# The MLP's first weights above the projection's buffers and ahead of its tables; three engines in program order to the MLP's end

## The chip, the cores and the metric

The kernel runs on one core of a Trainium2 chip. The metric is device time in microseconds (us), the median of a few runs. Beside it stands one profiled execution, whose trace lists every instruction on every engine with its start and its length.

The engines are named as the profile names them: PE is TensorE (matrix products, and transposes by a product with an identity), DVE is VectorE, ACT is ScalarE, POOL is GpSimd, SP is SyncE, which here does nothing but ask for DMA transfers. Each engine runs its own instruction list in order and waits at semaphores for the others. A "q" after an engine's name (DVEq, SPq) is its sequencer: branches, waits and requests for transfers. PSUM is the memory that PE writes its results into; a bank holds the result of one product.

## The reference

Two layers on an image of 48 x 48 tokens (2304) with 768 channels, all in float32. Layer 0 is a transformer block; layer 1 is a spectral mixing layer:

```python
# layer 0
xn = layernorm(x, ln1_g, ln1_b)
q, k, v = split(xn @ qkv_w + qkv_b)              # 12 heads of 64
attn = softmax(q*scale @ k^T + rel_h + rel_w)    # relative position along rows and columns
x = x + (attn @ v) @ proj_w + proj_b
h = gelu(layernorm(x, ln2_g, ln2_b) @ mlp_w1 + mlp_b1)      # 768 -> 3072
x = x + h @ mlp_w2 + mlp_b2                                 # 3072 -> 768
# layer 1
xf = rfft2(x, norm="ortho")                      # over the 48 x 48 tokens
o1 = relu(xf * w1 + b1); o2 = softshrink(o1 * w2 + b2, 0.01)  # complex, 8 blocks of 96 channels
y = irfft2(o2, norm="ortho") + x
```

The change touches the second half of layer 0: the projection `@ proj_w` with its residual, the second layer norm, and the MLP.

## The kernel before, in words

**Stages.** The program goes through layer norm with q, k and v, then attention, the projection, the MLP, and the spectral layer. The result of the first half, x1, stays on the chip as 18 tiles of 128 tokens. A program of this kind is written in Python as a list of operations with tiles from pools. A pool with `bufs=2` gives the same tile name two buffers in turn, and a third request waits for the last reader of the first. Pools opened inside a `with` give their memory back when it ends; a later pool that is laid in that memory waits for the readers of what was there. By default a scheduler decides the order of the instructions of each engine; inside `tc.manual_schedule(engines=...)` the engines named keep the order in which the program is written.

**Products by sevens.** Large products are done on 2 x 2 blocks with seven block products where eight are usual, at the price of sums of the operands. The helpers `left` (L158 to L168 with `right`) make the four sums of a left or right operand: `t1 = b12 - b11`, `t2 = b22 - t1` and so on. They run on GpSimd for the MLP's weights, on VectorE for its activations (`hs`), and on VectorE for the projection's activations (`sums_of_outputs`) and for the tokens that go into the MLP (`sums_of_tokens`, L170 to L177).

**The projection** (`projected`, L794 to L836). It goes over nine pairs u of token tiles. The attention's result `og` for a pair comes by DMA (`outputs`, L755). PE makes seven products of three matmuls each (L810) into four PSUM banks. ScalarE copies the first (pm1), VectorE adds it to the second (pu, L828) and the third (pu7, L832), GpSimd adds pu and pu7 into x1 (`first`, L820), and VectorE adds the other four products into x1 (`into`, L823). Pairs 0 to 3 run while a flag is tested that says whether the attention's short form of the softmax was safe. The branch on it is at L898. Pairs 4 to 8, the late projection, come after it. There the second layer norm of the first six token tiles is done too (`normalise`, L121 to L129: statistics on VectorE, a square root on ScalarE, then VectorE), their transposes (`transposed`: PE at L139, three transposes to a PSUM buffer, two buffers, read by ScalarE at L141 and VectorE at L145 in turn), and the addition of the MLP's second bias by GpSimd. The scheduler is free in all of this.

**The MLP.** Three passes p over 768 tokens each, and in a pass 12 blocks n of 256 hidden features. `hidden(p, n)` loads the block's w1 (L1147) and w2 (L1154, 768 KB each) by requests on SP, has GpSimd make the sums of both (eight operations), and makes seven products into four PSUM banks `h0` to `h3` (L1170). ScalarE copies the first (m1, L1189), VectorE adds (u, u7 and three c, L1182), ScalarE applies GELU (L1176), and VectorE makes the four sums `hs` of the result. `added(p, n, i)`, for three token groups i, makes seven single products with w2 (L1230, L1234) into banks `o0` to `o3`, which VectorE adds into x1 and into an accumulator (L1232 to L1238). The weights come from a pool with two buffers. The second half of block n-1, `added(p, n-1, i)`, is written between the parts of `hidden(p, n)`. The layer norm of the next pass's six tiles (`normalised`) is written at blocks 4 to 9; at the end of a pass come its transposes (`turned`), `sums_of_tokens` and the first step of the Fourier transform (`rows_forward`, L1262 to L1275). All of the MLP holds PE to program order; the other engines are free. Ahead of the first weights SP asks for two tables, b2 (L1133) and rows_dft (L1135).

Of the kernel before, what the change touches and what calls it, by code (L numbers as in the profile page):

```python
# [10 lines left out]
F32 = mybir.dt.float32  # L11
# [8 lines left out]
P = 128  # L20
HW = 48
T = HW * HW
# [7 lines left out]
TB = 768  # L30
G = 384
# [15 lines left out]
def block_then_afno(  # L47
# [26 lines left out]
    nc = tc.nc  # L74
# [39 lines left out]
    xt = shared[:, : NC * TB].rearrange("p (c t) -> p c t", c=NC)  # L114
# [78 lines left out]
    with ExitStack() as flag_scope:  # L193
# [557 lines left out]
        def outputs(u, pool, og=None):  # L751

            if og is None:
                og = pool.tile([P, NC, 2, P], F32, name="og", bufs=2)
            nc.sync.dma_start(  # L755
                out=og.rearrange("p c j t -> p c (j t)"),
                in_=oT[:, ts(u, 2 * P)].rearrange("(c p) t -> p c t", p=P),
            )
            return og
# [35 lines left out]
        def projected(psum, pool, u, og, sums):  # L795

            b11, b21, t3, b22 = (og[:, ds(3 * i, 3), j] for j in range(2) for i in range(2))
            t1, t2, t4 = (sums[:, i] for i in range(3))
            a11, a12, s3, a22 = weight_parts()
            s1, s2, s4 = (pws[:, i] for i in range(3))  # L800
            pairs_of = {
                1: (b11, a11), 2: (b21, a12), 3: (b22, s4), 4: (t4, a22),
                5: (t1, s1), 6: (t2, s2), 7: (t3, s3),
            }
            bank = [psum.tile([P, G], F32, name=f"m{i}") for i in range(4)]

            def product(i, k, first):
                a, b = pairs_of[k]
                for c in range(3):
                    nc.tensor.matmul(  # L810
                        bank[i], a[:, c, :], b[:, c, :], start=(first and c == 0),
                        stop=(c == 2), skip_group_check=not first,
                    )
                return bank[i]

            def half(j, k):
                return x1[:, 2 * u + j, ts(k, CH)]

            def first(j, k, src):
                nc.gpsimd.tensor_tensor(half(j, k), half(j, k), src, ALU.add)  # L820

            def into(j, k, src):
                nc.vector.tensor_tensor(half(j, k), src, half(j, k), ALU.add)  # L823

            m1 = pool.tile([P, G], F32, name="pm1")
            nc.scalar.copy(m1, product(0, 1, True))
            v = pool.tile([P, G], F32, name="pu")
            nc.vector.tensor_tensor(v, product(1, 6, True), m1, ALU.add)  # L828
            first(0, 1, v)
            first(1, 0, v)  # L830
            v7 = pool.tile([P, G], F32, name="pu7")
            nc.vector.tensor_tensor(v7, product(2, 7, True), v, ALU.add)  # L832
            first(1, 1, v7)
            into(1, 1, product(3, 5, True))
            into(0, 0, product(0, 2, False))
            into(0, 1, product(2, 4, False))  # L836
            into(1, 0, product(3, 3, False))
# [60 lines left out]
        with tc.If(safe < 1):  # L898
# [178 lines left out]
            with tc.tile_pool(name="g_ps_proj", bufs=2, space=PSUM) as psum, tc.tile_pool(  # L1077
# [9 lines left out]
                for i in range(4):  # L1087
                    sum_of_weights(i)

        with tc.tile_pool(name="ps_proj", bufs=1, space=PSUM) as psum, tc.tile_pool(  # L1090
            name="ps_turn", bufs=2, space=PSUM
        ) as psum_turn, tc.tile_pool(name="proj_late", bufs=2) as pl:
            hats, ogs = [], {EARLY: sums_of_outputs(pl, kept[EARLY])}
            for u in range(EARLY, PAIRS):
                if u + 1 < PAIRS:
                    if u + 1 not in kept:
                        kept[u + 1] = outputs(u + 1, pl)
                    ogs[u + 1] = sums_of_outputs(pl, kept[u + 1])
                projected(psum, pl, u, kept[u], ogs.pop(u))
                n = u - EARLY  # L1100
                if n in (2, 3):
                    transposed(
                        psum_turn, hats[3 * (n - 2) :][:3], xt, n - 2, V_LN2G, V_LN2B, tag="t"
                    )
                if n == 3:
                    sums_of_tokens(xt, xs)
                if n < 3:
                    for t in (2 * n, 2 * n + 1):
                        hats.append(normalise(ln2, x1[:, t, :]))
                        nc.gpsimd.tensor_tensor(x1[:, t, :], x1[:, t, :], b2, ALU.add)  # L1110
# [19 lines left out]
    with ExitStack() as mlp:  # L1130
        bias = mlp.enter_context(tc.tile_pool(name="mlp_const", bufs=1))
        b2 = bias.tile([P, C], F32, name="b2")
        nc.sync.dma_start(out=b2, in_=mlp_b2[0, :].partition_broadcast(P))  # L1133
        rows_dft = bias.tile([P, 3, 8, 64], F32, name="rows_dft")
        nc.sync.dma_start(out=rows_dft, in_=c_rows)  # L1135

        psum = mlp.enter_context(tc.tile_pool(name="ps_mlp", bufs=1, space=PSUM))
        hpool = mlp.enter_context(tc.tile_pool(name="mlp_h", bufs=2))
        upool = mlp.enter_context(tc.tile_pool(name="mlp_u", bufs=2))
        wpool = mlp.enter_context(tc.tile_pool(name="mlp_w", bufs=2))  # L1140
        n_f = FF // FCH
        kept = {}

        def hidden(p, n):

            w = wpool.tile([P, NC, FCH], F32, name="w1")
            nc.sync.dma_start(  # L1147
# [11 lines left out]
                nc.gpsimd, v[:, 0, :CH], v[:, 0, CH:], v[:, 1, :CH], v[:, 1, CH:],  # L1159
                [vs[:, i] for i in range(3)],  # L1160
            )
            h = hpool.tile([P, 2, TB], F32, name="hT")
            hs = hpool.tile([P, 3, G], F32, name="hs", bufs=1)
            kept[p, n] = h, hs, v, vs
# [116 lines left out]
        def normalised(p, i):  # L1281

            t = 6 * p + i
            hats[i] = turn.tile([P, C], F32, name="hat2", tag="turn")
            normalise(upool, x1[:, t, :], hats[i])
            nc.gpsimd.tensor_tensor(x1[:, t, :], x1[:, t, :], b2, ALU.add)  # L1286

        def turned(piece):

            for i in range(4 * piece, 4 * piece + 4):  # L1290
                j, c = divmod(i, NC)
                tp = psum.tile([P, G], F32, name="tp2", tag=f"h{i % 4}")
                for k in range(3):
                    nc.tensor.transpose(tp[:, ts(k, P)], hats[3 * j + k][:, ts(c, P)], ident)
                nc.scalar.activation(
                    xt[:, c, ts(j, G)], tp, AF.Identity, bias=col(V_LN2B + c), scale=col(V_LN2G + c)
                )

        with tc.manual_schedule(engines={mybir.EngineType.PE}):
            for p in range(T // TB):  # L1300
                for n in range(n_f):
                    work = hidden(p, n)
                    for i in range(3):
                        next(work)
                        if n:
                            added(p, n - 1, i)
                    if p < 2 and 4 <= n < 10:
                        normalised(p + 1, n - 4)
                for i in range(3):
                    if p < 2:  # L1310
                        turned(i)
                    added(p, n_f - 1, i)
                if p < 2:
                    sums_of_tokens(xt, xs)
                rows_forward(p)

    with ExitStack() as sp:
        psum = sp.enter_context(tc.tile_pool(name="ps_spec", bufs=2, space=PSUM))
# [380 lines left out]
```

## Time and profile before

| | us |
|---|---|
| median of three runs (2856.51 to 2860.92) | 2859.09 |
| profiled execution | 2857.95 |
| its span, first instruction to last | 2856.1 |
| PE busy | 2797.9 |
| DVE busy | 1734.3 |
| ACT busy | 915.6 |
| POOL busy | 651.7 |

PE's mean granted clock is 0.996 of full speed. By stage, from the windows view of the trace:

| stretch of the span, us | stage | PE busy |
|---|---|---|
| 0 to 480 | layer norm, q, k, v | 460.5 |
| 480 to 1430 | attention | 950 |
| 1430 to 1492.3 | projection of pairs 0 to 3, flag | 57.8 |
| 1492.3 to 1566.5 | late projection, pairs 4 to 8 | 73.9 |
| 1566.5 to 1576.3 | border to the MLP | 0.06 |
| 1576.3 to 1601.3 | first blocks of the MLP | 24.1 |
| 1601.3 to 2570 | the rest of the MLP | 963.0 |
| 2570 to 2856.1 | spectral layer | 268.5 |

How to read the profile: a row of instructions has the source line, the engine and operation, and the tiles it writes and reads as `out<-in` with their sizes. A row in brackets, `[9.74 <-DMA w]`, gives the idle time ahead of the instruction on its engine and what ended it. The list of waits gives, for each kind of waiting instruction and its releaser, the total, the number of times and the longest. Matmuls overlap, so three matmuls that make one product are best counted from the start of one product to the start of the next. The records' names of PE's matmuls into `h`, `o` and `m` are the PSUM banks of the MLP's first half, its second half, and the projection.

### The profile page before, as it was taken

What the parts mean: (1) busy time and instruction counts of PE and PEld (TensorE: products, weight loads), DVE (VectorE), ACT (ScalarE), POOL (GpSimd) and SP (SyncE); (2) the same over time, 40 slices, a digit from 0 to 9 for tenths busy, and PEclk for the clock granted to TensorE, in tenths of its full rate; (3) what the DMA queues carried; (4) which work ended last, traced back from release to release, by engine and by line L of the source; (5) the groups of instructions that cost most, each with busy time, mean ns of one, the idle gap of its engine ahead of it and who ended that gap; (6) DMA issues with size and microseconds to landing.
All of it is one profiled execution on the core that took longest, in us unless ns stands there. A gap on an engine that the chain in (4) does not pass through costs nothing. (4 is left out here: it accounts for less than half of the span.)

```text
span 2856.1 us, 41310 instructions
## 1 busy us (share of the span) xinstructions
PE 2797.9 (98%) x15829; PEld 1724.1 (60%) x15829; DVE 1734.3 (61%) x2540; ACT 915.6 (32%) x1470; POOL 651.7 (23%) x650
## 2 busy tenths in 40 slices
PE   8999999999999999999999999999999999999998
PEld 5555655656566656565555555555555555556887
DVE  5343226666666666676756666675666566666665
ACT  1011125657566666565501101121011211102332
POOL 2303010000000000000063532242232323222433
PEclk9999999999999999999999999999999999999999
DMA  4423275374573736546240221121121212113254
GB/s 150 132 99 111 93 164 108 62 134 79 88 141 52 135 60 113 115 73 100 94 175 21 85 66 59 52 91 62 46 67 56 89 56 66 49 61 112 61 161 141
DMA packets 216494, 262.79 MB, mean 92 GB/s; under 512 B 24524, under 2 KB 196908, under 8 KB 214752
## 3 DMA queue, kind: packets, MB, share of 16 engines
q1 hardware_dynamic: 213784, 258.03, 36.4%
q8 instruction: 127, 2.08, 0.3%
q10 hardware_dynamic: 2440, 1.84, 0.2%
q14 instruction: 79, 0.65, 0.1%
q0 software_dynamic: 64, 0.20, 0.0%
HBM read 143.96 MB, written 52.31 MB: 69 GB/s over the span
## 5 line engine op out<-in xcount | busy, mean ns | idle before, releaser
L581 ACT ACTIVATE main<-sp 128x768 f32<-128x768 f32 x648 | 516.5, 812 | 34.0 <-PE sp L571 19.3
L725 DVE TENSOR_TENSOR pairs<-pairs,main 128x1536 f32<-128x1536 f32 x252 | 443.1, 1758 | 27.2 <-DVE pairs L725 0.9
L571 PE MATMUL sp<-terms,select 64*128 64x384 f32 x1296 | 413.5, 630 | 0.0
L1232 DVE TENSOR_TENSOR main<-o,main 128x384 f32<-128x384 f32 x540 | 298.5, 556 | 39.5 <-PE o L1230 1.7
L1170 PE MATMUL h<-shared,w 128*128 128x384 f32 x864 | 298.0, 488 | 9.7 <-DMA w<-in_mlp_w_dram 9.7
L562 PE MATMUL sp<-shared 64*128 64x384 f32 x1296 | 266.9, 487 | 2.2 <-DVE o L462 2.2
L562 PE MATMUL sp<-qT,kT 64*128 64x384 f32 x1296 | 264.1, 484 | 0.0
L451 PE MATMUL m<-main 128*128 128x384 f32 x756 | 246.8, 488 | 2.7 <-DVE main L177 2.1
L1170 PEld LDWEIGHTS h<-shared,w 128*128 128x128 f32 x864 | 164.6, 191 | 125.9 <-POOL main L1286 10.3
L1170 PE MATMUL h<-shared,w1s 128*128 128x384 f32 x648 | 226.8, 486 | 0.4 <-POOL w1s L160 0.4
L627 POOL TENSOR_TENSOR inverse<-inverse,rden 24x32 f32<-24x32 f32 x36 | 15.2, 422 | 929.1 <-DVE sums L626 887.5
L1176 ACT ACTIVATE hT<-c,vec 128x384 f32<-128x384 f32 x108 | 66.4, 615 | 477.1 <-DVE c L1182 477.1
L594 PE MATMUL op<-main,shared 128*64 128x384 f32 x1296 | 217.4, 488 | 0.0
L594 PE MATMUL op<-main,v 128*64 128x384 f32 x1296 | 216.4, 488 | 0.0
L725 DVE TENSOR_TENSOR pairs<-main 128x1536 f32<-128x1536 f32 x36 | 63.3, 1758 | 247.3 <-ACT main L581 247.3
L451 PEld LDWEIGHTS m<-main 128*128 128x128 f32 x756 | 143.4, 191 | 103.7 <-issue 4.8
L1182 DVE TENSOR_TENSOR c<-h,u 128x384 f32<-128x384 f32 x108 | 60.2, 558 | 218.4 <-PE h L1170 218.4
L1230 PE MATMUL o<-w2s,hs 128*128 128x384 f32 x432 | 174.9, 487 | 2.3 <-DVE hs L160 2.3
L571 PEld LDWEIGHTS sp<-terms,select 64*128 64x128 f32 x1296 | 126.1, 187 | 83.7 <-issue 0.5
L1230 PE MATMUL o<-w,hT 128*128 128x384 f32 x432 | 175.1, 487 | 1.4 <-DVE acc L1238 0.7
L1170 PEld LDWEIGHTS h<-shared,w1s 128*128 128x128 f32 x648 | 123.0, 190 | 86.7 <-POOL w1s L160 1.2
L159 POOL TENSOR_TENSOR w1s<-w 128x384 f32<-128x384 f32 x36 | 36.9, 1024 | 547.0 <-DMA w<-in_mlp_w_dram 416.4
(187 smaller groups left out, 4033.8 us busy)
## 6 DMA issues: line engine op xcount, KB each, us to landing
w<-in_mlp_w_dram SPq DMA_DIRECT2D x72, 768.0 KB
terms<-col_parts SPq DMA_DIRECT2D x432, 72.0 KB
terms<-row_hi SPq DMA_DIRECT2D x216, 72.0 KB
terms<-row_lo SPq DMA_DIRECT2D x216, 72.0 KB
main<-in_qkv_w_dram SPq DMA_DIRECT2D x36, 384.0 KB
z<-zt SPq DMA_DIRECT2D x48, 192.0 KB
x<-in_x_blocks_dram SPq DMA_DIRECT2D x18, 384.0 KB
k_d<-o SPq DMA_DIRECT2D x36, 192.0 KB
```

The lines of the kernel that those rows point to most:

```text
L159: eng.tensor_tensor(s[0], a21, a22, ALU.add)
L451: nc.tensor.matmul(bank, a[:, c, :], b[:, c, :], start=(first and c == 0), stop=(c == 2), skip_group_check=not first,)
L562: nc.tensor.matmul(sp[:, j, :G], kT[at, ts(kt, P)], qT[at, ts(c, G)], start=first, stop=not first,)
L571: nc.tensor.matmul(sp[:, j, :G], select[at, a % 2], ready[pr, c][at, a // 2, b], start=first, stop=not first,)
L581: nc.scalar.activation(p, sp[:, :, :G], AF.Exp, scale=HD**-0.5)
L594: nc.tensor.matmul(op[ts(j, 64)], v[:, kt, ts(j, 64)], exps[:, kt, j, :], start=(kt == 0), stop=(kt == NT - 1),)
L725: nc.vector.tensor_tensor(pairs, so_far, exps[:, ds(kt - 1, 2)], ALU.add)
L1170: nc.tensor.matmul(bank[i], a[:, c, :], b[:, c, :], start=(start and c == 0), stop=(c == 2), skip_group_check=not start,)
L1176: nc.scalar.activation(h[:, i, ts(k, G)], src, AF.Gelu, bias=col(V_B1 + 2 * n + i))
L1182: nc.vector.tensor_tensor(t, src, other, ALU.add)
L1230: nc.tensor.matmul(bank[k], a, b, start=start, stop=True, skip_group_check=not start)
L1232: nc.vector.tensor_tensor(dst, bank[k], dst, ALU.add)
```

## The change

Five edits. In the late projection pm1, pu and pu7 get one buffer each in place of two, and `og` of u = 6 to 8 comes from the pool `pj` (which also holds u = 4 and 5, two buffers) and no longer from `proj_late`. A manual schedule of PE, POOL and SP opens ahead of the late projection and closes behind the MLP, in place of the one of PE alone around the MLP. A pool `apart` with one tile that nobody uses is put below the weights' pool, so that this pool lies above the projection's buffers. The loads and sums of a block's weights leave `hidden` for a function `weights(p, n)`; it is called for (0, 0) ahead of the loop, for the next block behind the products of a block, and for the first two blocks of the next pass behind `sums_of_tokens`. The requests for b2 and rows_dft move from ahead of the MLP to block (0, 2).

```diff
--- before.py
+++ after.py
@@ -822,13 +822,13 @@
             def into(j, k, src):
                 nc.vector.tensor_tensor(half(j, k), src, half(j, k), ALU.add)
 
-            m1 = pool.tile([P, G], F32, name="pm1")
+            m1 = pool.tile([P, G], F32, name="pm1", bufs=1)
             nc.scalar.copy(m1, product(0, 1, True))
-            v = pool.tile([P, G], F32, name="pu")
+            v = pool.tile([P, G], F32, name="pu", bufs=1)
             nc.vector.tensor_tensor(v, product(1, 6, True), m1, ALU.add)
             first(0, 1, v)
             first(1, 0, v)
-            v7 = pool.tile([P, G], F32, name="pu7")
+            v7 = pool.tile([P, G], F32, name="pu7", bufs=1)
             nc.vector.tensor_tensor(v7, product(2, 7, True), v, ALU.add)
             first(1, 1, v7)
             into(1, 1, product(3, 5, True))
@@ -1087,6 +1087,12 @@
                 for i in range(4):
                     sum_of_weights(i)
 
+        in_order = ExitStack()
+        in_order.enter_context(
+            tc.manual_schedule(
+                engines={mybir.EngineType.PE, mybir.EngineType.Pool, mybir.EngineType.SP}
+            )
+        )
         with tc.tile_pool(name="ps_proj", bufs=1, space=PSUM) as psum, tc.tile_pool(
             name="ps_turn", bufs=2, space=PSUM
         ) as psum_turn, tc.tile_pool(name="proj_late", bufs=2) as pl:
@@ -1094,7 +1100,7 @@
             for u in range(EARLY, PAIRS):
                 if u + 1 < PAIRS:
                     if u + 1 not in kept:
-                        kept[u + 1] = outputs(u + 1, pl)
+                        kept[u + 1] = outputs(u + 1, pj)
                     ogs[u + 1] = sums_of_outputs(pl, kept[u + 1])
                 projected(psum, pl, u, kept[u], ogs.pop(u))
                 n = u - EARLY
@@ -1130,18 +1136,20 @@
     with ExitStack() as mlp:
         bias = mlp.enter_context(tc.tile_pool(name="mlp_const", bufs=1))
         b2 = bias.tile([P, C], F32, name="b2")
-        nc.sync.dma_start(out=b2, in_=mlp_b2[0, :].partition_broadcast(P))
         rows_dft = bias.tile([P, 3, 8, 64], F32, name="rows_dft")
-        nc.sync.dma_start(out=rows_dft, in_=c_rows)
 
         psum = mlp.enter_context(tc.tile_pool(name="ps_mlp", bufs=1, space=PSUM))
         hpool = mlp.enter_context(tc.tile_pool(name="mlp_h", bufs=2))
         upool = mlp.enter_context(tc.tile_pool(name="mlp_u", bufs=2))
+        apart = mlp.enter_context(tc.tile_pool(name="apart", bufs=1))
+        apart.tile([P, 560], F32, name="apart")
         wpool = mlp.enter_context(tc.tile_pool(name="mlp_w", bufs=2))
         n_f = FF // FCH
         kept = {}
 
-        def hidden(p, n):
+        ready_w = {}
+
+        def weights(p, n):
 
             w = wpool.tile([P, NC, FCH], F32, name="w1")
             nc.sync.dma_start(
@@ -1159,6 +1167,11 @@
                 nc.gpsimd, v[:, 0, :CH], v[:, 0, CH:], v[:, 1, :CH], v[:, 1, CH:],
                 [vs[:, i] for i in range(3)],
             )
+            ready_w[p, n] = a11, a12, a21, a22, ws, v, vs
+
+        def hidden(p, n):
+
+            a11, a12, a21, a22, ws, v, vs = ready_w.pop((p, n))
             h = hpool.tile([P, 2, TB], F32, name="hT")
             hs = hpool.tile([P, 3, G], F32, name="hs", bufs=1)
             kept[p, n] = h, hs, v, vs
@@ -1296,23 +1309,31 @@
                     xt[:, c, ts(j, G)], tp, AF.Identity, bias=col(V_LN2B + c), scale=col(V_LN2G + c)
                 )
 
-        with tc.manual_schedule(engines={mybir.EngineType.PE}):
-            for p in range(T // TB):
-                for n in range(n_f):
-                    work = hidden(p, n)
-                    for i in range(3):
-                        next(work)
-                        if n:
-                            added(p, n - 1, i)
-                    if p < 2 and 4 <= n < 10:
-                        normalised(p + 1, n - 4)
+        weights(0, 0)
+        for p in range(T // TB):
+            for n in range(n_f):
+                if (p, n) == (0, 2):
+                    nc.sync.dma_start(out=b2, in_=mlp_b2[0, :].partition_broadcast(P))
+                    nc.sync.dma_start(out=rows_dft, in_=c_rows)
+                work = hidden(p, n)
                 for i in range(3):
-                    if p < 2:
-                        turned(i)
-                    added(p, n_f - 1, i)
+                    next(work)
+                    if n:
+                        added(p, n - 1, i)
+                if n < n_f - 1 and (p == 0 or n):
+                    weights(p, n + 1)
+                if p < 2 and 4 <= n < 10:
+                    normalised(p + 1, n - 4)
+            for i in range(3):
                 if p < 2:
-                    sums_of_tokens(xt, xs)
-                rows_forward(p)
+                    turned(i)
+                added(p, n_f - 1, i)
+            if p < 2:
+                sums_of_tokens(xt, xs)
+                for n in range(2):
+                    weights(p + 1, n)
+            rows_forward(p)
+        in_order.close()
 
     with ExitStack() as sp:
         psum = sp.enter_context(tc.tile_pool(name="ps_spec", bufs=2, space=PSUM))
```

In the changed file the first product of a block is at L1183, the loads of w1 and w2 at L1155 and L1162, GELU at L1189, the sums u and c at L1195, the copy m1 at L1202, the products of the second half at L1243 and L1247, VectorE's additions of them at L1245 to L1251, and the two tables at L1316 and L1317.

## The prediction

> **What bounds the kernel now.** I read the page first: TensorE (PE) is busy for 2797.9 of 2856.1 us, so a gain must come out of the 58 us in which it waits, or out of time in which it runs slowly. Next I listed whom PE waits for (engine, line, releaser: total, times, longest):
>
> ```profile
> PE h L1170 <- DMA w<-in_mlp_w_dram: 9.7, 1, 9.7
> PE m L810 <- DVEq L898: 4.0, 1, 4.0
> PE o L1230 <- DVE main L1232: 3.3, 4, 1.3
> ```
>
> The first is one wait, at the border between the projection and the MLP. PE's timeline there (start, length, work; in brackets the idle time before it and its releaser):
>
> ```profile
> 1564.40 2.10 PE L810 MATMUL m<-pws,og 128*128 128x384 f32 x6
> 1576.24 3.58 PE L1170 MATMUL h<-shared,w 128*128 128x384 f32 x6 [9.74 <-DMA w<-in_mlp_w_dram]
> 1580.25 2.20 PE L1170 MATMUL h<-shared,w1s 128*128 128x384 f32 x6 [0.44 <-POOL w1s L160]
> 1582.29 2.10 PE L1170 MATMUL h<-shared,w 128*128 128x384 f32 x6
> ```
>
> A group of three products (6 records) starts every 1.94 us (1580.25 to 1582.29 and on). The first group after the wait takes 3.58 us and is followed by 0.44 us more. The windows view has a granted clock of 0.50 from 1570 to 1578, so the slow group belongs to the wait. Why the weights come late is in SP's timeline:
>
> ```profile
> 1492.28 43.03 SPq L755 DMA_DIRECT2D og<-oT  x3
> 1566.60 0.35 SPq L1133 DMA_DIRECT2D b<-in_mlp_b_dram  x1
> 1567.00 0.42 SPq L1135 DMA_DIRECT2D rows_dft<-in_c_rows_dram  x1
> 1567.62 0.38 SPq L1147 DMA_DIRECT2D w<-in_mlp_w_dram  x1
> ```
>
> SP asks for nothing between 1535 and 1566.60, then for 1.2 MB of tables, and only then for the first w1. Its longest wait there is L1133 on PE L810, 31.2 us: memory of the projection.
>
> **What the Trainium skill says.** (1) "TensorE: Matmul & The Clock Gate", Part 1: the clock halves after an idle window of about 3.4 us and comes back after as much work. The trace agrees (0.50 in the wait). New pauses below 3 us should not bring it back. (2) "SBUF — State Buffer", Who interferes with whom: a VectorE instruction with two SBUF inputs contends with a GpSimd instruction that reads SBUF. The trace agrees: the same 128x384 `hs` sum takes 0.56 us in one place and 1.35 in another. (3) "ScalarE: Activation LUTs", What ACT_TABLE_LOAD costs: 1283 ns for each change of table; the trace has 1.28.
>
> **The change, part by part.** u counts pairs of token tiles in the projection (4 to 8 stand here), (p,n) blocks of the MLP. I follow the instruction order of the changed kernel as built and give everything in us of the profile before.
>
> *First weights.* The first w1 load now waits for nothing of its own; it stands behind og of u=8 on SP's queue, which goes out at about 1535, when u=6 ends. Before, five loads asked for from 1566.60 on kept the DMA at 345 to 399 GB/s, so 768 KB takes about 2.1 and the first lands some 4.3 after it is asked for. og keeps its place; the four weight loads behind it are there by 1548. GpSimd makes their sums after its last projection addition, L820. That ends at 1563.5 before, about 1564 now, and w1s for the second group needs the first two sums (1.31 + 0.99). It is ready before PE comes. If PE went straight on, group two would start at 1564.40 + 2 x 1.94 = 1568.28 and not at 1580.25. **Removable: 11.97.** The tables b2 and rows_dft go behind block (0,2)'s weights; their first readers come at n=4 and after p=0, some 60 and 330 later: nothing.
>
> *A wait that appears.* PE's first MLP product takes the PSUM bank that the last projection result leaves, and so waits for the last L823: 1566.54 + 0.56, plus 0.15 for the signal (1598.20 + 0.54 to 1598.89 in another place), 1567.25 against 1566.34. **Lost: 0.91.** Before, this lay under the DMA wait.
>
> *Program order on PE.* The one change in PE's order is in the transposes of the layer norm (L139), 18 for each of two sets. Before, the scheduler put projection products among them:
>
> ```profile
> 1534.76 0.82 PE L139 MATMUL tp<-ident,hat 128*128 128x128 f32 x6
> 1535.41 1.46 PE L810 MATMUL m<-col_parts,og 128*128 128x384 f32 x4
> 1536.70 0.82 PE L139 MATMUL tp<-ident,hat 128*128 128x128 f32 x6
> 1537.23 0.68 DVE L145 TENSOR_SCALAR shared<-tp,vec 128x384 f32<-128x384 f32 x1 [1.13 <-PE tp L139]
> ```
>
> Now the 18 stand together on two PSUM buffers. Three transposes (0.33) fill one. It is read from 0.53 after their start (1536.70 to 1537.23), for 0.67, and is free 0.15 later: 1.35 a round. The third filling ends at 2 x 1.35 + 0.33 + 0.33 (the other buffer follows) = 3.36, and not at 18 x 0.108 = 1.95. **Lost: 2 x 1.4 = 2.8.** What is late next: nothing, since the delay gives VectorE time and removes PE's wait of 0.25 for L832. **Won: 0.25.** Bounds: 0.9 to 1.6 a set.
>
> *og in pj.* og of u=6 and u=7 now waits for the end of u=4 and u=5: asked for at 1507.9 and 1521.4, landed at 1512.2 and 1525.7. Before, u=6 and u=7 were asked for at once after 1492. The sums (four VectorE operations) now stand between L828 and L832 of the pair before. For u=5: L828 at 1512.5 to 1513.0, four sums of 1.9 without and 5.6 with GpSimd's contention (1540.3 to 1546.3 has it), L832 at 1515.4 to 1519. PE needs that at 1517.3. GpSimd is then busy for only two additions (1.94), so I take **0.3 lost**, bounds 0 and 2. For u=6 PE's need is at 1530.9 and the late end 1531: nothing. One buffer for pm1, pu, pu7: the reader of each is done over 7 before the next write.
>
> *Layer norm of p=1 on VectorE.* This work (six tiles, hoisted by the scheduler, 1567 to 1582.5) lay in PE's wait. That cover is gone. As built, it now stands among block (0,0)'s own VectorE work, with one square root after another, and ScalarE's table changes between square root and GELU five times where it changed once: 4 x 1.28 more. With D the end of the last L823: two tiles take to D+5.8 (2.08 each with GpSimd busy, as at 1573.05, 1575.13, 1577.21), u to 6.3, u7 to 7.9, the first c to 10.45. PE needs it at D+11.7: block (0,0) runs without a stop. The last two GELUs come at 14.9 and 15.8 (behind two table loads), and hs begins at D+16.6 where PE ends its first groups of (0,1) at 17.5. Before, the four hs sums lay so:
>
> ```profile
> 1594.04 1.24 DVE L160 TENSOR_TENSOR hs<-hs,hT 128x384 f32<-128x384 f32 x1
> 1595.19 1.35 DVE L162 TENSOR_TENSOR hT<-hT 128x384 f32<-128x384 f32 x1
> 1596.46 1.35 DVE L161 TENSOR_TENSOR hs<-hT,hs 128x384 f32<-128x384 f32 x1
> 1598.89 0.89 PE L1230 MATMUL o<-w,hT 128*128 128x384 f32 x2 [0.31 <-DVE acc L1236]
> ```
>
> With these lengths L161 ends at about D+20.8; then a held-back layer norm (L129, 0.66), u and the copy of the first result reach 22.6, and PE's fifth product of the set waits for that copy. PE should be there at 20.1, after 0.5 + 0.5 for L160 and L162. Two more additions and a statistic keep it back by some 0.5 + 0.4. The set ends at about D+25.2 instead of 22.0: 3.2. The same set cost 1601.33 - 1595.84 - 7 x 0.645 = 0.98 before. **Lost: 2.2 more.** Bounds: with uncontended sums 0.85 in all, so a gain of 0.1; with every operation at its contended length 5.6, so 4.6 lost.
>
> *Later blocks.* w1 of block n+1 is asked for right behind w2 of block n. 4.3 + 2.1 to land and eight GpSimd operations of 1.0 to 1.3 end some 15 into a block of 27.1 (1609.7 to 1636.8): nothing while that holds. GpSimd's b2 additions move from the ends of p to n=4 to 9, at most one of 1.8 a block. PE's waits on VectorE at the ends of p (about 4 in all) may move by 1 either way; I take nothing.
>
> **Sum:** 11.97 - 0.91 - 2.8 + 0.25 - 0.3 - 2.2 = 6.0 gained. The profiled execution took 2857.95 (span 2856.1 and 1.85 around it), so 2851.9. The median of the runs, 2859.09, lies 1.1 above it: 2853.1. About 0.2%, 5.7 us, is what a measurement of this kernel can tell from no change, and the forecast lies on that line.
>
> **Rivals.** *The VectorE queue is lighter than I take it.* If GpSimd's sums rarely meet VectorE's, the hs set costs 0.85 and the transposes 1.1 a set: 6.0 + 2.3 + 0.6 = 8.9, 2850. For it: hs sums of 0.55 in the same table. Against: GpSimd makes block (0,2)'s sums just then. *It is heavier:* 4.6 for hs and 2 for og of u=6: 6.0 - 2.4 - 1.7 = 1.9, 2857. For it: 1540 to 1546 shows such lengths. *Slower, through the later weights.* One queue position decides: if landing and sums took over 27.1 a block, each of some 33 blocks would start late. From 17.7/33 = 0.54 late a block the kernel passes 0.2% slower; 1 late gives 2859.1 - 6.0 + 33 = 2886. For it: program order holds SP and GpSimd, where the old order ran ahead by up to two blocks. Against: 12 of slack. *The first load still waits*, for memory or a queue: then 11.97 stays and the losses of 3 show, 2862. Against: its list of waits.
>
> **How the numbers follow.** The sum with its middle bounds, a gain of 4.5 to 7.5: 0.43. Lighter, gain over 7.5: 0.27. Heavier, gain under 4.5: 0.24. Later weights 0.04, first load late 0.02. Of the first case 0.25 lies beyond 5.7. Faster: 0.25 + 0.27 = 0.52. Slower: 0.05, nearly all of the last two. Same: 0.43. The range reaches to the lighter case's 2850 less 2 and up to the heavier one's 2857 and a little: 2848 to 2857.5. The likeliest case alone has 2851.6 to 2854.6.
>
> **What would show it.** Right: SP asks for w1 at 1535 to 1537; PE's first L1170 group (L1183 after) starts within 1.5 of its last L810, at full clock, released by VectorE's L823; two groups of 18 transposes of 3.2 to 3.5; the first set of `o` products of (0,1) with 2 to 5 of waiting for hs and acc; five table loads near 1580 to 1592. Wrong: a wait for w over 1 in any block, a pause of PE above 3.4 with a lower clock, waits at L832 of u=5 over 1, or a first set of `o` without waits.

## The result and the profile after

The changed kernel takes 2848.11 us (median of 8 runs, 2845.63 to 2850.48), the kernel before 2857.48 (median of 8, 2853.71 to 2860.92). The ratio is 0.9967, with a 95% interval from 0.9956 to 0.9978: faster by 6.3 to 12.6 us, with 9.4 us, a third of a per cent, between the medians. The forecast was 6.0 faster, 2853.1 us, with a range from 2848.0 to 2857.5. Of the 5.0 us between forecast and median, 1.6 come from the starting level: the forecast stood on three runs of the kernel before with a median of 2859.09. The other 3.4 are gain that the sum didn't have.

The profiled execution has a span of 2844.9 us; before it was 2856.1. The first part of its page, busy time by engine:

```profile
PE 2794.3 (98%) x15829; PEld 1722.6 (61%) x15829; DVE 1699.3 (60%) x2540; ACT 920.4 (32%) x1474; POOL 643.5 (23%) x650
```

PE is busy 3.6 us less with the same number of instructions, VectorE 35 us less. VectorE does the same work, so its instructions became shorter. That is a first sign of less contention with GpSimd, and of where the unforeseen gain lies. The list of PE's waits (who waits, for whom: total, times, longest):

```profile
PE m L810 <- DVEq L898: 3.8, 1, 3.8
...
PE tp L139 <- DVE shared L145: 2.0, 4, 0.6
PE o L1243 <- DVE hs L160: 2.0, 2, 1.1
PE o L1243 <- DVE mv L123: 1.5, 1, 1.5
...
PE h L1183 <- POOL w2s L165: 0.7, 1, 0.7
```

The wait of 9.7 for the first w1 is gone. In its place stand 0.7 at the first MLP group, four short waits of the transposes, and a wait of 1.5 in the first set of second products. PE's timeline shows these three places:

```profile
1551.13 0.82 PE L139 MATMUL tp<-ident,hat 128*128 128x128 f32 x6
1552.53 0.88 PE L139 MATMUL tp<-ident,hat 128*128 128x128 f32 x6 [0.58 <-DVE shared L145]
1553.84 0.87 PE L139 MATMUL tp<-ident,hat 128*128 128x128 f32 x6 [0.44 <-DVE shared L145]
...
1566.17 2.10 PE L810 MATMUL m<-pws,og 128*128 128x384 f32 x6
1568.96 2.17 PE L1183 MATMUL h<-shared,w 128*128 128x384 f32 x6 [0.70 <-POOL w2s L165]
...
1592.52 0.88 PE L1243 MATMUL o<-w,hT 128*128 128x384 f32 x2 [1.52 <-DVE mv L123]
```

The transposes take 3.43 a set (1551.13 to the next product at 1554.55). The first MLP group starts 2.79 after the last L810 group and runs at full clock. In SP's timeline the first w1 is asked for at 1534.81, behind og of u = 8:

```profile
1534.81 0.49 SPq L1155 DMA_DIRECT2D w<-in_mlp_w_dram  x1
```

I cut both executions into stretches at the same instructions of PE. Each is a difference of two starts, so what happened ahead of a stretch doesn't enter it:

| stretch | before | after | won | in the forecast |
|---|---|---|---|---|
| late projection: first L810 group to last | 72.05 | 74.42 | -2.37 | -2.85 |
| last L810 group to second MLP group | 15.85 | 4.80 | 11.05 | 11.06 |
| from there to the first second product | 15.59 | 15.48 | 0.11 | 0 |
| first set of second products, (0,1) | 5.49 | 8.84 | -3.35 | -2.2 |
| the other blocks of pass 0 | 283.16 | 283.15 | 0.01 | 0 |
| end of pass 0: last group of first products to the first second product of pass 1 | 60.78 | 58.16 | 2.62 | 0 |
| end of pass 1, likewise | 57.36 | 56.12 | 1.24 | 0 |
| all else from pass 1 to the spectral layer | 611.08 | 611.08 | 0 | 0 |

The first two groups behind the branch took 5.64 in both executions, so the first row is not disturbed by the clock there. The sum is 9.31, beside 9.37 between the medians. The spans differ by 11.2. The rest, 0.60 ahead of the branch and 1.30 in the spectral layer, is no part of the change: the spectral part took 242.39 before, 241.09 after, and 240.8 to 243.7 in the experiments, none of which touches it.

### The profile page after: what moved, and what is told of

It reads as the page before. It is cut to its first block, busy times and chain, and to the rows that moved or that the text cites. A ratio compares the mean times of both kernels' runs of the same rounds, so it can differ in the third digit from the quotient of the medians.

```text
span 2844.9 us, 41192 instructions
## 1 busy us (share of the span) xinstructions
PE 2794.3 (98%) x15829; PEld 1722.6 (61%) x15829; DVE 1699.3 (60%) x2540; ACT 920.4 (32%) x1474; POOL 643.5 (23%) x650
## 5 line engine op out<-in xcount | busy, mean ns | idle before, releaser
L1245 DVE TENSOR_TENSOR main<-o,main 128x384 f32<-128x384 f32 x540 | 299.0, 556 | 38.5 <-PE o L1243 0.3
L1183 PE MATMUL h<-shared,w 128*128 128x384 f32 x864 | 296.6, 486 | 0.7 <-POOL w2s L165 0.7
L1183 PEld LDWEIGHTS h<-shared,w 128*128 128x128 f32 x864 | 163.9, 190 | 116.2 <-POOL w2s L165 1.3
L1183 PE MATMUL h<-shared,w1s 128*128 128x384 f32 x648 | 226.7, 486 | 0.0
L1189 ACT ACTIVATE hT<-c,vec 128x384 f32<-128x384 f32 x108 | 66.5, 615 | 464.5 <-DVE c L1195 464.5
L1195 DVE TENSOR_TENSOR c<-h,u 128x384 f32<-128x384 f32 x108 | 60.2, 557 | 212.4 <-PE h L1183 212.4
L1243 PE MATMUL o<-w2s,hs 128*128 128x384 f32 x432 | 174.9, 487 | 2.0 <-DVE hs L160 2.0
L1243 PE MATMUL o<-w,hT 128*128 128x384 f32 x432 | 174.9, 486 | 1.9 <-DVE mv L123 1.5
L1183 PEld LDWEIGHTS h<-shared,w1s 128*128 128x128 f32 x648 | 123.1, 190 | 85.9
L165 POOL TENSOR_TENSOR w2s<-w 128x384 f32<-128x384 f32 x36 | 36.0, 1000 | 566.2 <-DMA w<-in_mlp_w_dram 350.1
```

The costliest lines, as they stand in the source:

```text
L1183: nc.tensor.matmul(bank[i], a[:, c, :], b[:, c, :], start=(start and c == 0), stop=(c == 2), skip_group_check=not start,)
L1189: nc.scalar.activation(h[:, i, ts(k, G)], src, AF.Gelu, bias=col(V_B1 + 2 * n + i))
L1195: nc.vector.tensor_tensor(t, src, other, ALU.add)
L1243: nc.tensor.matmul(bank[k], a, b, start=start, stop=True, skip_group_check=not start)
L1245: nc.vector.tensor_tensor(dst, bank[k], dst, ALU.add)
```

## The experiments

All are the changed kernel with one edit. The times of single runs are spans of profiled executions; the changed kernel has 2844.9. Spans differ without an edit: the changed kernel's eight executions have 2843.5 to 2848.4. The first products after the branch come at a changing clock (two groups took 3.97 to 6.91 us in the runs here), and the spectral layer differs as said. So I compare stretches, as in the table above.

### The gain at the passes' ends: who slowed VectorE before

In the kernel before, VectorE's timeline has hs of block n = 11 at the end of pass 0:

```profile
1891.21 1.32 DVE L159 TENSOR_TENSOR hs<-hT 128x384 f32<-128x384 f32 x1 [0.16 <-PE o L1230]
1892.45 0.55 DVE L1232 TENSOR_TENSOR main<-o,main 128x384 f32<-128x384 f32 x1
1892.92 0.88 DVE L160 TENSOR_TENSOR hs<-hs,hT 128x384 f32<-128x384 f32 x1
```

The sum that comes out of PSUM between them (L1232) has its usual 0.55; the sums of two SBUF tiles are long. GpSimd's timeline of the same kernel says what ran beside them, the weight sums of block (1,0), from 1889 on:

```profile
1889.07 1.00 POOL L159 TENSOR_TENSOR w1s<-w 128x384 f32<-128x384 f32 x1 [16.37 <-DMA w<-in_mlp_w_dram]
```

In the changed kernel GpSimd begins these sums at 1910.52, after the pass's last additions, and VectorE's hs has its short form:

```profile
1885.16 0.56 DVE L159 TENSOR_TENSOR hs<-hT 128x384 f32<-128x384 f32 x1 [0.16 <-PE o L1243]
1885.64 0.55 DVE L1245 TENSOR_TENSOR main<-o,main 128x384 f32<-128x384 f32 x1
1886.10 0.55 DVE L160 TENSOR_TENSOR hs<-hs,hT 128x384 f32<-128x384 f32 x1
```

The first test puts one block's weight sums back ahead of the pass's end:

```diff
+            if p < 2:
+                weights(p + 1, 0)
             for i in range(3):
                 if p < 2:
                     turned(i)
                 added(p, n_f - 1, i)
             if p < 2:
                 sums_of_tokens(xt, xs)
-                for n in range(2):
-                    weights(p + 1, n)
+                weights(p + 1, 1)
```

> The changed kernel, but the weights of block (p+1,0) are loaded and summed ahead of a pass's last additions and not behind them. Theory: the 3.9 us that the changed kernel won at the ends of passes 0 and 1 come from GpSimd having nothing to sum while VectorE makes hs of block n = 11. Then GpSimd's eight sums stand at the end of the pass again, the first two hs sums there take about 1.3 and 0.9 us in place of 0.56 and 0.55, PE waits some 0.9 for hs, and the stretch from the first set of products of (0,11)'s last but one group to (1,0)'s first goes from 56.2 us back towards 58.8; pass 1's from 54.2 towards 55.4. Rival: the gain comes from the second bias's additions, which left the end of the pass; then the stretches stay within 0.4 of 56.2 and 54.2.

Measured: span 2845.8. The end of pass 0 took 58.91 (58.16 in the changed kernel, 60.78 before), that of pass 1 56.13 (56.12 in the changed kernel). GpSimd's four sums of w1 ran earlier than I meant, and the four of w2 at 1889.49 to 1894.1, after hs, which kept 0.55. So the test missed hs. What it did hit is the next set of second products, where VectorE's L1259, a sum of two SBUF tiles, took 1.09 in place of 0.56: that set lasted 6.25, against 5.50 in the changed kernel and 6.19 before. Neither theory had this number: the rival's bound of 0.4 is passed at pass 0 and holds at pass 1.

The second test goes for hs itself. GpSimd makes four additions in the unused tile, the first of which waits for VectorE's last additions of block n = 10:

```diff
+            for i in range(4):
+                if p < 2:
+                    src = spare[:, :CH] if i else x1[:, 6 * p + 2, :CH]
+                    nc.gpsimd.tensor_tensor(spare[:, :CH], src, src, ALU.add)
             for i in range(3):
                 if p < 2:
                     turned(i)
```

> The changed kernel with four additions of 128x384 by GpSimd in the unused tile at the ends of passes 0 and 1, beginning when VectorE has added the last group of block n = 10, that is just before it makes hs of n = 11. Nothing reads what they write. Theory: GpSimd's reading of SBUF slows VectorE's sums with two SBUF inputs, so hs (0.55 to 0.56 us each now) takes 0.9 to 1.35 us in at least two of four, PE waits 0.7 to 1.3 for hs at each of the two ends (no wait there now), and the kernel is 1 to 2.5 us slower: this was the kernel before's wait of 0.89. Rival: hs stays at 0.55 us and no wait comes back; then the gain at the passes' ends has another cause, the order of VectorE's work.

Measured: span 2850.3; the ends of passes 59.52 and 57.46, so 1.36 and 1.34 slower. (The other 2.7 of the span lie nearly all in the spectral layer, which had its longest time here.) VectorE's timeline at pass 0:

```profile
1886.08 0.71 DVE L160 TENSOR_TENSOR hs<-hs,hT 128x384 f32<-128x384 f32 x1
1886.71 1.18 DVE L162 TENSOR_TENSOR hT<-hT 128x384 f32<-128x384 f32 x1
1887.81 1.18 DVE L161 TENSOR_TENSOR hs<-hT,hs 128x384 f32<-128x384 f32 x1
```

The theory holds in its main point: GpSimd's work alone, which nobody reads, lengthens hs and costs PE 1.36 in one set (5.90 against 4.54). PE's timeline shows only 0.22 and 0.15 of it as idle time, less than I expected; the rest stands as later starts of single products, 0.66 to 1.10 apart and not 0.645. The 2.62 of pass 0 can now be laid out by sets: 1.10 in the first (4.54 against 5.64 before; the second test makes 1.36), 0.69 in the next (the first test makes 0.75), 0.42 in the last, and 0.41 in the Fourier products. The 1.24 of pass 1 lies in its first set (4.54 against 5.77 before), where the second test makes 1.34. So for the first set of both passes GpSimd's sums are shown as the cause, and for the next set of pass 0 they are shown to make as much. The last two parts were not tested. A rival stands for them: in the kernel before, GpSimd's additions of the second bias ran in this stretch (1902.43 to 1906.01, at the end of that next set, and 1920.40 to 1931.41), and they too have left it.

### The border: memory and the queue's order

The first run takes out the unused tile, so that the weights' pool reaches into the projection's memory:

```diff
-        apart = mlp.enter_context(tc.tile_pool(name="apart", bufs=1))
-        apart.tile([P, 560], F32, name="apart")
```

> The changed kernel without the unused tile, so that the weights' buffers reach 2,240 bytes into the projection's memory. The first w1 load then waits for the next to last group of products of u = 8 (L810 that reads ogs). Theory, that order ahead of the tables is the larger part: it is asked for when that group ends, lands some 4.3 us later, PE pauses about 4.5 us in place of 2.8 between the start of the last L810 group and the first MLP group, and the second group, behind two GpSimd sums, starts 6.5 to 8 us after the last L810 group (4.80 now, 15.85 before): 2 to 3 us lost of the 11. Rival, that the memory is the larger part: more than 6 us lost.

Measured: span 2849.4. From the last L810 group to the first MLP group 4.89, to the second 8.38: 3.6 lost at the border, of which 1.3 came back in the first set of second products (7.52 for 8.84). That the memory is the smaller part holds, but 8.38 lies just above the 6.5 to 8 that I gave. PE's timeline says why:

```profile
1572.76 3.70 PE L1181 MATMUL h<-shared,w 128*128 128x384 f32 x6 [2.79 <-DVE stats L121]
1576.25 2.31 PE L1181 MATMUL h<-shared,w1s 128*128 128x384 f32 x6
```

The first group is at a low clock (the windows view has 0.50 from 1574 to 1576), after a pause of 2.79 only. (The releaser named, VectorE's statistic, need not be the cause: the load was asked for at 1568.18 and its parts landed up to 1572.56, 0.20 before PE started.)

The second run asks for the two tables ahead of the first weights again:

```diff
                 if (p, n) == (0, 2):
-                    nc.sync.dma_start(out=b2, in_=mlp_b2[0, :].partition_broadcast(P))
-                    nc.sync.dma_start(out=rows_dft, in_=c_rows)
...
+        nc.sync.dma_start(out=b2, in_=mlp_b2[0, :].partition_broadcast(P))
+        nc.sync.dma_start(out=rows_dft, in_=c_rows)
         weights(0, 0)
```

> The changed kernel with the loads of b2 and rows_dft put back ahead of the first weights; these stay above the projection's buffers. The tables lie in the projection's memory and wait for its last product, and SP keeps program order. Theory: SP stands at b2 until then, w1 comes as late as in the kernel before, and the second MLP group starts 15 to 16 us after the last L810 group (4.80 now, 15.85 before): the whole 11 is lost, which says that neither half of the edit is worth anything without the queue's order. Rival: w1 is late only by the tables' own transfer, 1.2 MB at about 350 GB/s, 3.5 us.

Measured: span 2850.8, 15.27 to the second MLP group, as the theory said; the list of PE's waits has the old wait again:

```profile
PE h L1183 <- DMA w<-in_mlp_w_dram: 9.4, 1, 9.4
```

SP asks for b2 at 1568.46 and for w1 at 1569.34, though w1's memory is the same that was free for a load at 1534.81 in the changed kernel. But only 5.9 of the 10.5 us show in the span. The first set of second products took 4.51 here, and 8.84 in the changed kernel: with PE waiting, the layer norm of pass 1 has its cover again. So the first weights' move was worth 10.5 at the border and lost 4.3 of it one block later, 6.1 net.

### The first set: where the layer norm of pass 1 stands

Three runs hold it back to blocks 4 to 9. In the first, GpSimd rewrites one column of a tile, in program order, where the layer norm is written:

```diff
             hats[i] = turn.tile([P, C], F32, name="hat2", tag="turn")
+            if p == 1:
+                nc.gpsimd.tensor_copy(x1[:, t, 0:1], x1[:, t, 0:1])
             normalise(upool, x1[:, t, :], hats[i])
```

> The changed kernel, with the layer norm of pass 1 held back to blocks 4 to 9 (GpSimd rewrites one column of each tile with itself in program order, and the layer norm reads the tile after that). Theory: this layer norm, among block (0,0)'s own work on VectorE and with its changes of ScalarE's table, is what makes the first set of second products late; that set then takes 5.0 to 5.6 us (8.84 now, 5.49 in the kernel before), and about 3.3 us are won there. Rival one: hs is late by contention with GpSimd's weight sums alone; then the set still takes over 7. Rival two: the table changes only move (two a tile, at blocks 4 to 9), PE waits there for hs or c, and of the 3.3 less than half is left.

Measured: span 2871.8. The first set took 4.52, so the theory's half is right, 4.3 won. But PE waited 17.8 for VectorE in the second products of blocks 4 to 9 (21.1 in the whole MLP), and these blocks became 29.8 longer, also because the clock fell to 0.50 there four times. It is neither rival. VectorE's list of waits and GpSimd's timeline show another queue:

```profile
DVE stats L121 <- POOL main L1299: 19.3, 6, 3.8
```

```profile
1700.12 0.99 POOL L168 TENSOR_TENSOR w<-w 128x384 f32<-128x384 f32 x1
1701.06 0.18 POOL L1299 COPY main<-main 128x1 f32<-128x1 f32 x1
```

The rewriting stood on GpSimd behind sums that waited for w2. VectorE stood at the statistic that waits for the rewriting, and the additions of PE's results, behind it in VectorE's order, came late. The second run moves the rewriting to the start of the block:

```diff
+                if p == 0 and 4 <= n < 10:
+                    t = 6 + n - 4
+                    nc.gpsimd.tensor_copy(x1[:, t, 0:1], x1[:, t, 0:1])
                 work = hidden(p, n)
```

> The changed kernel with pass 1's layer norm held to blocks 4 to 9 again, but GpSimd's rewriting of a column stands at the start of a block, ahead of the weight sums that wait for the load of w2. Theory: the 21 us lost in the run before came from VectorE standing at a statistic (L121) behind that rewriting, which stood on GpSimd's queue behind sums waiting for w2. With it ahead of them, the first set of second products keeps its 4.5 us (8.84 in the changed kernel), waits at blocks 4 to 9 fall from 21 to under 2 in all, and the kernel is 2.5 to 4.5 us faster than the changed one. Rival: the table changes of ScalarE (two a block) hold VectorE at the reciprocal, and PE still waits over 1 us a block.

Measured: span 2876.7, first set 4.52 again, waits of 22.7 in blocks 4 to 9 (26.1 in the whole MLP), and 36.7 more time in these blocks. I had missed that the sums of the block's own w2 wait on that queue too: the start of a block is still behind them (VectorE waited 24.3 in all, six times, for the rewriting at L1320). The third run takes GpSimd out of it; ScalarE rewrites the column behind the block's third GELU:

```diff
+            if p == 1:
+                behind = kept[p - 1, i + 4][0][:, 1, 0:1]
+                first = x1[:, t, 0:1]
+                nc.scalar.activation(first, behind, AF.Identity, bias=first, scale=0.0)
             normalise(upool, x1[:, t, :], hats[i])
```

> The changed kernel with pass 1's layer norm held to blocks 4 to 9 by ScalarE: one column of a tile is rewritten as itself plus zero times a value of that block's third GELU, and the layer norm reads the tile after that. Nothing of it stands on GpSimd's queue. Theory: where the layer norm stands costs the 4.3 us of the first set of second products, and the 21 and 26 us of the two runs before were GpSimd's queue, not ScalarE's tables. Then that set takes 4.5 us (8.84 in the changed kernel), waits of PE in blocks 4 to 9 stay under 2 us in all, and the kernel is 2.5 to 4.5 us faster than the changed one. Rival: two changes of table a block hold the reciprocal on VectorE, and PE waits over 0.7 us a block, which takes all of it back.

Measured: span 2842.9, first set 4.51, from the first of these lines to the second, with no wait in it:

```profile
1586.13 0.81 PE L1247 MATMUL o<-w,hT 128*128 128x384 f32 x2
...
1590.64 0.81 PE L1183 MATMUL h<-shared,w 128*128 128x384 f32 x2
```

No wait of PE for VectorE is listed between 1600 and 1880. So the place of this layer norm was the cause of the loss in the first set, and the long waits of the two runs before were GpSimd's queue. The layer norm's VectorE work and its table loads moved together, so their shares are not shown. The new place isn't free of cost: the other blocks of pass 0 took 284.36 in place of 283.15, in slips of 0.06 to 0.42. Of the 4.3 won 3.1 is left, and 2.0 in the span, where the spectral layer took 1.0 longer.

### Program order in the late projection

This run opens the manual schedule only ahead of the first weights, so that the late projection is the scheduler's again:

```diff
-        in_order = ExitStack()
-        in_order.enter_context(
-            tc.manual_schedule(
-                engines={mybir.EngineType.PE, mybir.EngineType.Pool, mybir.EngineType.SP}
-            )
-        )
         with tc.tile_pool(name="ps_proj", bufs=1, space=PSUM) as psum, tc.tile_pool(
...
+        in_order = ExitStack()
+        in_order.enter_context(
+            tc.manual_schedule(
+                engines={mybir.EngineType.PE, mybir.EngineType.Pool, mybir.EngineType.SP}
+            )
+        )
         weights(0, 0)
```

> The changed kernel, with program order of the three engines only from the first weights on, so that the late projection is the scheduler's. It then puts transposes among products again, asks for the first four weight loads ahead of og of u = 6, and puts GpSimd's weight sums among the additions of u = 4. Theory: program order in the projection pays by keeping GpSimd's additions ahead of the weight sums. Without it GpSimd waits for weights that land some 6 us after the branch, the additions of pu and pu7 come 5 to 12 us late, VectorE's additions behind them too, and PE waits 4 to 10 us in u = 5 or 6; against it stand 2.9 from the transposes; in sum 2 to 7 us slower than the changed kernel. Rival: pairs have enough slack, no wait of PE over 1 us shows in the late projection, and the kernel is 2 to 3 us faster than the changed one.

Measured: span 2854.2, the late projection 84.48 in place of 74.42. Its list of waits:

```profile
PE m L810 <- DVE main L823: 7.3, 2, 7.2
...
PE m L810 <- DVE pu L832: 1.8, 2, 1.5
```

The kind of loss is the theory's, but its size is 9.3 by the span and not 2 to 7: 10.1 is lost in the late projection, and 2.9 is won in the first set, which took 5.96; the end of pass 0 and the spectral layer took 2.2 more. The pause of 7.2 also brings a low clock (4.21 and 2.90 for the next two groups). GpSimd's list has the sums of two blocks' weights among the additions of u = 4, and the additions of u = 5 come at 1524.58, some 12 late. Without program order in the projection the early weights lose there nearly all of the 11 that they win at the border; program order is what keeps GpSimd's additions first.

Program order also puts the 18 transposes of a set together. The next run gives them four buffers:

```diff
-            name="ps_turn", bufs=2, space=PSUM
+            name="ps_turn", bufs=4, space=PSUM
```

> The changed kernel with four PSUM buffers for the late projection's transposes in place of two. Theory: the 18 transposes of a set are slow only because each pair of buffers has to be read first; with four, a set takes about 1.95 to 2.1 us (3.43 now), the two waits for VectorE's L145 (0.58 and 0.44 a set) are gone, and 2.7 to 2.9 us are won. Rival: the readers are the limit (six readings of 0.67 us on two engines, 2.0 us), or the additions that stand behind them on VectorE come late and PE waits there; then less than 1.5 us is won.

Measured: span 2844.7. PE's timeline has the 18 transposes of a set in one piece:

```profile
1534.40 2.28 PE L139 MATMUL tp<-ident,hat 128*128 128x128 f32 x18
```

A set takes 2.12 (to the next product at 1536.52), and the late projection 71.79, 2.63 less. The span doesn't show it: the spectral layer took 1.1 longer, and the stretch at the end of pass 0 1.3. There the clock is at 0.50 from about 1902.9 to 1906.2, after waits of 0.43 and 1.62 that the changed kernel has too, at full clock.

### Both together

The last kernel has four buffers for the transposes and holds the layer norms of passes 1 and 2 to the blocks by ScalarE.

> The same for the layer norms of passes 1 and 2, and four PSUM buffers for the late projection's transposes: the version the runs point to. Expected against the changed kernel: 2.6 from the transposes, 4.3 from the first set, and 0 to 2 at the end of pass 0, where pass 2's layer norm no longer stands among VectorE's additions: 5 to 9 us faster than the changed kernel's 2848.1, so 2839 to 2843, a ratio to the kernel before of 0.9935 to 0.995. If the layer norm inside the blocks costs PE more than 0.5 a block, it comes out at 2843 to 2848.

Measured: 2840.26 us, median of 5 runs (2838.21 to 2842.41), beside 2856.78 for the kernel before (9 runs); ratio 0.994, interval 0.9926 to 0.9954. Its median lies 7.9 below the changed kernel's; with each set against its own runs of the kernel before, the gain is 16.5 beside 9.4. The first set takes 4.52, the end of pass 0 56.12 (58.16 in the changed kernel): without pass 2's layer norm among VectorE's additions another 2.0 is won.

## Why the prediction was right or wrong

*What bounds it, and the first weights: right.* SP asks at 1534.8 (forecast 1535), the wait for w1 is gone, and 11.05 is won at the border where 11.06 was forecast. The run with the tables in front shows the cause, the queue's order; the run without the unused tile gives the memory's own part, 3.6.

*The wait that appears: right.* 0.92 (4.80 less two groups of 1.94), forecast 0.91. The profile names GpSimd's w2s as releaser, but that sum ended at 1568.31, 0.65 before PE started. VectorE's last L823, which reads the bank, ended at 1568.86, 0.10 before, which fits the wait that was forecast.

*The transposes: right.* A set takes 3.43; before, it took 3.92 with a group of products of 1.94 in it, so 1.44 a set is lost, 2.88 in all, forecast 2.8. Four buffers take 2.63 of it back. *L832:* 0.51 won, with the product behind it, forecast 0.25. *og in pj:* no wait at L832 of u = 5 and none of u = 6, forecast 0.3 lost.

*The layer norm of pass 1 on VectorE: right in its mechanism, short in size.* Five table loads between 1578.9 and 1594.1, hs from 1585.92 on, PE kept back by the copy of the first result behind a held-back layer norm, all as forecast. The term was 2.2 more than before and measured 3.35, inside its bounds of 0.1 less and 4.6 more. (The prediction quotes the Trainium skill for 1283 ns a change of table. That is the load alone; the same section adds a drain of about 1380 ns. The trace sides with the smaller price: a square root ended at 1578.89, the load of 1.28 began at 1578.91 and the GELU at 1580.20.) VectorE's timeline:

```profile
1585.92 0.93 DVE L159 TENSOR_TENSOR hs<-hT 128x384 f32<-128x384 f32 x1
1586.88 1.23 DVE L160 TENSOR_TENSOR hs<-hs,hT 128x384 f32<-128x384 f32 x1
...
1591.83 0.55 DVE L1249 COPY acc<-o 128x384 f32<-128x384 f32 x1
```

With D = 1568.86 hs began 0.5 later and the copy ended 0.9 later than forecast (1592.38 and 1591.46), and the set's end slipped by 1.2. PE's fifth product of the set began at 1592.52, 0.14 behind that copy.

*The step that failed*, inside a range that held, is the last line of "Later blocks": "PE's waits on VectorE at the ends of p (about 4 in all) may move by 1 either way; I take nothing". The two ends gained 3.86. In the sentence before I followed GpSimd's bias additions to their new place, but not its weight sums at a pass's end, although they move by more: in program order they stand behind the last additions of the pass. Counted from the same set of products (1886.42 and 1880.38) they begin after 30.1 us, and after 2.65 in the kernel before. I had the contention of VectorE and GpSimd in hand, with its price, for the hs of block (0,0), and didn't ask where else it comes or goes.

*Luck in the number.* The median lies 0.1 above the lower end of the range. The range went that low for the rival "The VectorE queue is lighter" (2850), and that mechanism didn't happen: the hs set and the transposes cost more, not less. A gain at another place filled the gap, so that the range held is in part luck.

*The rivals.* The later weights held their slack: no wait for w in any block. A sum in this rival was wrong: with 6.0 gained, 0.2% slower is reached at 11.7/33 = 0.35 late a block; the 17.7 counts the removed wait alone, without the losses. One more sentence was wrong: "New pauses below 3 us should not bring it back" (the low clock). The run without the unused tile has 0.50 after a pause of 2.79; in the changed kernel no such pause is left beside the branch's.

## What to carry to other kernels

When an edit takes a wait away, ask what used that wait as its cover: here 10.5 us at the border gave 4.3 back one block later, and putting the covered work elsewhere won 3.1 of them again. When a queue goes into program order, follow every kind of instruction on it to its new neighbours, on other engines too, and price the contention that it leaves as carefully as the one that it brings. An instruction that others wait for doesn't belong on a queue behind a wait for DMA, however short it is.

## What was not expected of the hardware

- A sum of two SBUF tiles on VectorE, 0.55 us alone, took from 0.7 to 1.35 beside GpSimd's sums; an addition out of PSUM kept 0.54 to 0.56 beside them. "SBUF — State Buffer", Who interferes with whom, in the Trainium skill says that the former contend; that a short overlap of four additions of GpSimd costs PE 1.36 was new.
- The granted clock fell to 0.50 after a pause of PE of 2.79 us in one run. It also fell to 0.50, for 3.3 us or more, after waits of 0.43 and 1.62 in two runs (four buffers for the transposes; the late projection left to the scheduler), and in the first set of second products after waits of 1.09, 0.36 and 1.52 in the run with early sums; other runs kept the full clock after like waits. "TensorE: Matmul & The Clock Gate", Part 1, in the Trainium skill gives an idle window of about 3.4 us; these runs show lower clocks after less.
- After the branch, with pauses of 3.7 to 4.0, the first two groups of products took from 3.97 to 6.91 us in runs whose work there is the same.
